# A graph network layer on one core: gather buffers, the first attributes of a layer, and the banks of its completing products

## The chip, the core and the metric

The kernel runs on one core of a Trainium2 chip. The metric is the device time in microseconds (us) of one execution, and the median of three runs stands for it. The core's engines are TensorE (PE; its weight loads are listed as PEld), VectorE (DVE), ScalarE (ACT), GpSimd (POOL) and SyncE (SP). Each has its own instruction stream, and they wait for one another on semaphores. DMAs are issued from SyncE's and ScalarE's queues, and the gathers from GpSimd's.

## What is computed

There are 6250 nodes with 256 values each and 100000 edges, sorted by destination, with 32 attributes and one of three types. Three layers follow one another; at the end each row of input plus result is normalised. Cut to what matters:

```python
ew = edge_attr @ edge_w + edge_b
for l in range(3):
    residual = x
    msg = relu(x[src] * ew)
    out = zeros((n, 256))
    for i in range(3):
        h = segment_sum(msg * rel_masks[i][:, None], dst) * inv_cnt[i][:, None]
        out = out + h @ weights[l, i]
    out = out + x @ roots[l] + biases[l]
    x = residual + relu(out)
x = layernorm(x_in + x)
```

## The kernel before

A first stage looks at the destinations and decides, on the chip, between two paths; the inputs here take `ordered_path`. It splits the edges into 782 tiles of 128 edges. Two tiles are a pair (391 of them), and two pairs a quad. The pairs are worked in the order 64 to 390 and then 63 down to 0, so that the nodes of tiles 0 and 1, which take the edges of the pairs below 64, are finished last.

For a pair, GpSimd gathers the source rows of its two tiles (`gather_pair`, L928, two indirect DMAs of 128 rows of 1 KB). A quad's rows lie in one tile `xs`, which `room` gives out from the pool `rows` of ROWS = 8 buffers. TensorE makes the edge weights `ew_p` from the attributes (L623). VectorE multiplies the rows by them (`weigh`, L645), ScalarE takes the positive part (`bound`, L649), and VectorE builds comparisons of the edges' destinations with places (`one_hot`, L655). TensorE sums the messages by destination and type with them (`reduce`, L665, `h_p`), and VectorE adds the sums to the accumulator `acc` (`add`, L683). When the edges of a tile of 128 nodes are through, `node_mul` (L711) multiplies its sums by the layer's weights and `node_end` (L742 to L762) puts the result together with the root term in `x_root`. In layers 0 and 1 it writes the new rows to `x_mid` in DRAM (L747), from which the next layer gathers; in layer 2 they go to the output.

The order is written out by hand: the loop `for it in range(-11, max(starts) + 7)` issues for each step the pieces of many pairs at different distances. The step's gather is that of the pair AHEAD = 9 places on, `make_ew` that of 4 on, `weigh` that of 3 on, `reduce` its own. The scheduler keeps this order on each engine, so that only the semaphores set when an instruction begins.

The seam between two layers has pieces of its own. FIRST = 6 pairs of the next layer are gathered ahead (`gather_early`, 12 gathers), while node tile 0 of this layer isn't there yet: its rows are zero in `x_mid`. `complete` (L637 to L639) adds the missing rows in the next layer. It multiplies a comparison `came` of the source numbers with the 128 nodes of tile 0 by that tile's rows, and adds the product to `xs`; it does so once for each of the two pairs of the three quads. The 13th gather of a layer and all after it read `x_mid` with tile 0 in it, and so wait for its write. That write in turn overwrites what the early gathers read, and waits for them. In the first layer the six pairs are gathered from the input before the choice of path.

The attributes of eight pairs (a group) are one tile `at` of a pool of three. Layer 0 makes them by transposing `edge_attr` (`turn`, L607, `keep_attrs`, L615) and stores them in `at_all` (`store_at`, L599); layers 1 and 2 load them from there (`load_at`, L563, 512 KB each) on SyncE's queue. The first two groups of the next layer are loaded at the steps U and U + 1, where U = 391 is the number of pairs. The last `store_at` of layer 0 is issued at step U - 5, and the loads of the next layer's root matrix and biases (`load_root`) at U - 10.

The root terms (`root_turn`, L688, to `root_keep`, L699) are made some steps ahead of a node tile's turn, and kept in `x_root`, ROOTS = 24 places of 256 values for each partition. The place of the j-th node tile by turn is j modulo 24. PSUM has eight banks; the pools `o_p` and `r_p` have one each, and `h_p` and `ew_p` the rest with, in layer 0, `turn_p`. `complete` uses `o_p` for both of its products. `r_p` serves the root terms, and the second half of node tiles 0 and 1.

Of the kernel before, what the change touches and what calls it, by code (L numbers as in the profile page):

```python
# [8 lines left out]
F32 = mybir.dt.float32  # L9
# [430 lines left out]


@with_exitstack
def ordered_path(ctx, tc, x, edge_attr, weights, roots, biases, edge_w, edge_b, out, src, src_i, seg, place_i, consts, rows,
                 first_rows, node_i):


# [4 lines left out]
    P = 128  # L451
    N, D = x.shape
    E, A = edge_attr.shape
    L, R = weights.shape[:2]
# [3 lines left out]
    U = T // 2  # L458
# [14 lines left out]
    ident, ones, iota_w = consts  # L473
# [6 lines left out]
    big = ctx.enter_context(tc.tile_pool(name="big", bufs=1))  # L480
# [3 lines left out]
        nc.scalar.dma_start(ew_sb[row + A:row + A1, :], edge_b[None, :])  # L484

    x_all = big.tile([P, NT, D], F32, name="x_all")
    x_root = big.tile([P, ROOTS, D], F32, name="x_root")


    acc = big.tile([P, DC + 1, R, ASIDE + 2 * P + WIN], F32, name="acc")  # L490
# [23 lines left out]
    came_i = came.bitcast(I32)  # L514

    edge = ctx.enter_context(tc.tile_pool(name="edge", bufs=2))
    wpool = ctx.enter_context(tc.tile_pool(name="wpool", bufs=1))
    o_pool = ctx.enter_context(tc.tile_pool(name="o_p", bufs=1, space=PSUM))
    r_pool = ctx.enter_context(tc.tile_pool(name="r_p", bufs=1, space=PSUM))

    groups = list(dict.fromkeys(u // 4 for u in order))
    at_groups = list(dict.fromkeys(u // GROUP for u in order))
# [34 lines left out]
    def pairs_in(g):  # L557
        return min(GROUP, U - GROUP * g)

    def load_at(l, g):  # L560
        at = edge.tile([P, GROUP, P], F32, name="at", bufs=3)
        if l > 0:
            nc.sync.dma_start(at[:, :pairs_in(g)].rearrange("p k e -> p (k e)"), at_all[g, :, :pairs_in(g) * P])  # L563
        return at

    def find_came():
        e = 2 * P * order[0]
        nc.scalar.dma_start(came_i.rearrange("p t e -> p (t e)"),
                            src[e:e + 2 * FIRST * P][None, :].to_broadcast([P, 2 * FIRST * P]))
        for t in range(2 * FIRST):  # L570
            nc.vector.tensor_scalar(came[:, t, :], came_i[:, t, :], node_i[:, 0:1], None, op0=ALU.is_equal)

    def layer(l, r_sb, b_sb, ats, early, pools):
# [13 lines left out]
        r_next, ats_next, early_next = (None, None), {}, {}  # L587

        def gather(u):
            p = order.index(u)  # L590
            if p < FIRST:
                xs[u // 2] = early[u // 2]
            else:
                if first_of(p, 2):
                    xs[u // 2] = room(rows, D)
                gather_pair(nc, xs[u // 2], x_rows, src_i, u)
# [4 lines left out]
        def pairs_of(q):  # L601
            return range(min(2, U - 2 * q))
# [24 lines left out]
        def gather_early(p):  # L627
            u = order[p]
            if first_of(p, 2):
                early_next[u // 2] = room(rows, D)  # L630
            gather_pair(nc, early_next[u // 2], x_mid[l], src_i, u)

        def complete(q):
            for k in pairs_of(q):
                rest = o_pool.tile([P, 2, D], F32, name="o_p")
                for i in range(2):
                    nc.tensor.matmul(rest[:, i, :], came[:, 4 * q + 2 * k + i - 2 * order[0], :], x_all[:, 0, :],  # L637
                                     start=True, stop=True)
                nc.vector.tensor_add(xs[q][:, k], rest, xs[q][:, k])  # L639
# [132 lines left out]

        node_at = {s: c for c, s in enumerate(starts)}
        turns_of = [node_at[s] for s in sorted(node_at)]
        at_root = {c: j % ROOTS for j, c in enumerate(turns_of)}
        root_at = {}

        for j, c in enumerate(turns_of):
# [5 lines left out]
        for it in range(-11, max(starts) + 7):  # L784
            def pair(k):
                return order[it + k] if 0 <= it + k < U else None
            if pair(AHEAD) is not None:
                gather(pair(AHEAD))
            if l < L - 1 and 0 <= it + AHEAD - U < FIRST:
                gather_early(it + AHEAD - U)  # L790
            if l == 0 and it == 20:
                find_came()
            if l == 0 and pair(11) is not None and first_of(it + 11, 4):
                load_attrs(pair(11) // 4)
            if l > 0 and pair(AHEAD) is not None and pair(AHEAD) // GROUP not in ats:
                ats[pair(AHEAD) // GROUP] = load_at(l, pair(AHEAD) // GROUP)
            if l == 0 and it >= -4 and (it + 4) % 20 == 0 and (it + 4) // 20 * 6 < NT - 1:
                load_x((it + 4) // 20 * 6)
            if it == 10:
                nc.sync.dma_start(w_sb, weights[l].rearrange("r (c p) e -> p (r c) e", p=P))  # L800
            if l == L - 1 and it + 2 in root_at:
                load_x0(root_at[it + 2])
            if l < L - 1 and it == U - 10:
                r_next = load_root(l + 1)
            if l < L - 1 and U <= it < U + 2:
                ats_next[at_groups[it - U]] = load_at(l + 1, at_groups[it - U])

            if pair(4) is not None and first_of(it + 4, 2):
                make_ew(pair(4) // 2)
            if pair(0) is not None:  # L810
                reduce(pair(0))
            if pair(-LAG) is not None:
                add(pair(-LAG))
            if pair(3) is not None and first_of(it + 3, 2):
                if l > 0 and it + 3 < FIRST:
                    complete(pair(3) // 2)
                weigh(pair(3) // 2)
                bound(pair(3) // 2)
            if l == 0:

                for k, work in ((6, keep_attrs), (7, turn)):
                    if pair(k) is not None and first_of(it + k, 2):
                        work(pair(k) // 2)
                if pair(4) is not None and last_of(it + 4, GROUP):
                    store_at(pair(4) // GROUP)
            if it in root_at:
                root_turn(root_at[it])
            if it - 1 in root_at:
                root_turned(root_at[it - 1])
            if it - 2 in root_at:  # L830
                root_mul(root_at[it - 2])
            if it - 3 in root_at:
                root_keep(root_at[it - 3])
            if it == moved:
                move()
            if it - 2 == moved:
                clear(P)
            if it + 1 in node_at and slot_of(node_at[it + 1]) == 0:
                wrap()
            if it in node_at:  # L840
                node_mul(node_at[it], 0)
            if it - 1 in node_at:
                node_end(node_at[it - 1], 0)
            if it - 2 in node_at:
                node_mul(node_at[it - 2], 1)
            if it - 3 in node_at:
                node_end(node_at[it - 3], 1)
                clear(slot_of(node_at[it - 3]))
            if it - 4 in node_at and l == L - 1:
                deviate(node_at[it - 4])  # L850
            if it - 5 in node_at and l == L - 1:
                norm(node_at[it - 5])
            if pair(2) is not None and first_of(it + 2, 2):
                one_hot(pair(2) // 2)
# [15 lines left out]
ROOTS = 24  # L870
GROUP = 8
ROWS = 8
FIRST = 6
# [47 lines left out]
def room(rows, D):  # L921

    return rows.tile([128, 2, 2, D], F32, name="xs", bufs=ROWS)
# [10 lines left out]
def kernel(ctx, tc, x, src, dst, edge_attr, edge_type, weights, roots, biases, edge_w,  # L934
# [4 lines left out]
    P = 128  # L939
    N, D = x.shape  # L940
# [7 lines left out]
    U = T // 2  # L948
# [3 lines left out]
    keep = ctx.enter_context(tc.tile_pool(name="keep", bufs=1))  # L952
    ident = keep.tile([P, P], F32, name="ident_o")
    make_identity(nc, ident)
    ones = keep.tile([1, P], F32, name="ones_o")
    nc.vector.memset(ones, 1.0)
    iota_w = keep.tile([P, WK], F32, name="iota_w")
    nc.gpsimd.iota(iota_w, pattern=[[1, WK]], base=0, channel_multiplier=0,
                   allow_small_or_imprecise_dtypes=True)
    node_i = keep.tile([P, 1], F32, name="node_i")  # L960
    nc.gpsimd.iota(node_i, pattern=[[0, 1]], base=0, channel_multiplier=1, allow_small_or_imprecise_dtypes=True)
    src_i = keep.tile([P, TC], I32, name="src_io")
    seg = keep.tile([P, TC], F32, name="seg_o")
    place_i = keep.tile([1, (U + 1) // 2], I32, name="place_i")
    flag = keep.tile([1, 1], I32, name="flag")
    rows = ctx.enter_context(tc.tile_pool(name="rows", bufs=ROWS))

    with tc.tile_pool(name="look", bufs=1) as look, tc.tile_pool(name="look_p", bufs=2, space=PSUM) as look_p, \
            tc.manual_schedule():
        full, rest = divmod(E, P * J)  # L970
# [46 lines left out]
        first_rows = {}  # L1017
        for u in schedule(N, E, 1)[0][:FIRST]:
            if u // 2 not in first_rows:
                first_rows[u // 2] = room(rows, D)  # L1020
            gather_pair(nc, first_rows[u // 2], x, src_i, u)
        dst_t = by_tile("dst")

# [47 lines left out]
    unordered = nc.values_load(flag[0:1, 0:1], min_val=0, max_val=1)  # L1071
    with tc.If(unordered == 0):
        ordered_path(tc, x, edge_attr, weights, roots, biases, edge_w, edge_b, out, src, src_i, seg, place_i,
                     (ident, ones, iota_w), rows, first_rows, node_i)
    with tc.If(unordered > 0):
        general_path(tc, x, src, dst, edge_attr, edge_type, weights, roots, biases, edge_w, edge_b, out)

# [25 lines left out]
```

## Time and profile before

| | us |
|---|---|
| median of 3 runs | 3021.46 (3019.87 to 3021.53) |
| the profiled execution, its own time | 3018.21 |
| its span, first to last instruction | 3016.4 |
| TensorE busy | 2789.6 (92%) |
| GpSimd busy | 2236.2 (74%) |
| VectorE busy | 2080.6 (69%) |
| ScalarE busy | 987.1 (33%) |
| mean granted TensorE clock | 0.942 of full speed |

The profile is of one execution. Its page gives the busy time of each engine, the span in 40 slices with the granted TensorE clock, the chain of work that ended last, and the costliest groups of instructions: line, engine, operation, output<-inputs, count, then the busy time, the mean of one in ns, the idle time ahead of it on its engine, and what ended most of that. "issue" there means that the trace shows nothing that was waited for. The timeline lists instructions in order: start, duration, engine, line, what they write and read, how many are merged (x4), and in brackets the idle time before and what ended it. SPq is an instruction of SyncE's queue that issues a DMA. Most instructions of TensorE are listed in pieces, so that a product in float32 counts as two. The layers run to about 1020, about 2010 and the end.

The waits are also told by who waited for whom. Over the span, ScalarE's L649 waited 1792.3 us for VectorE's L645, L645 waited 362.0 us for gathers from `x_mid` and 97.6 us for gathers from the input, and TensorE's L623 waited 149.2 us for L645.

### The profile page before, as it was taken

The numbers are of one execution on the slowest core, as the hardware profiler recorded it, in microseconds if no ns is written. First come the engines' busy times: TensorE is split into PE (matmuls) and PEld (weight loads), VectorE is DVE, ScalarE is ACT, GpSimd is POOL, SyncE is SP. The second block draws the span as 40 slices with busy tenths as digits, with TensorE's granted clock in tenths as the row PEclk, the third lists the DMA queues.
The fourth block names the chain that finished last, engine by engine and source line by source line (L and its number), as shares of the span: only waits on it lengthen the run. The fifth ranks groups of instructions, "written<-read, shape, count | busy, mean of one in ns | idle before, by whom it ended". The sixth has DMA issues, their size and how long they took to land.

```text
span 3016.4 us, 55782 instructions
## 1 busy us (share of the span) xinstructions
PE 2789.6 (92%) x18114; PEld 2252.3 (75%) x18114; DVE 2080.6 (69%) x5865; ACT 987.1 (33%) x1354; POOL 2236.2 (74%) x2355
## 2 busy tenths in 40 slices
PE   6899999999999889999999999889999999999997
PEld 5777878888877667777777777667777777777775
DVE  6676767777776556666666667556667777877765
ACT  4444444444444222222222222212222222322221
POOL 6777777777777677777777777767777777777775
PEclk9999999999999899999999999878999999999888
DMA  5655555555555444444444445434554444444443
GB/s 154 176 162 161 166 165 151 149 158 156 159 156 145 144 125 137 139 132 140 134 142 144 144 137 149 151 116 140 151 149 146 147 147 149 142 144 144 135 139 97
DMA packets 274682, 438.87 MB, mean 145 GB/s; under 512 B 145004, under 2 KB 180032, under 8 KB 274384
## 3 DMA queue, kind: packets, MB, share of 16 engines
q0 software_dynamic: 112608, 307.65, 35.1%
q1 hardware_dynamic: 154720, 119.64, 13.4%
q10 hardware_dynamic: 7056, 7.92, 0.9%
q8 instruction: 149, 2.44, 0.3%
q14 instruction: 149, 1.22, 0.1%
HBM read 389.94 MB, written 45.09 MB: 144 GB/s over the span
## 4 chain that ended last, share of the span: by engine, by line
PE 56%; DMA 16%; POOL 10%; issue 8%; DVE 7%; ACT 2%; DVEq 0%; ACTq 0%; POOLq 0%; SPq 0%
PE h_p L665 25%; PE ew_p L623 16%; DMA xs<-x_mid,src_io 12%; POOL xs L928 10%; PE o_p L711 9%; DVE xs L645 4%; DMA xs<-in_x_dram,src_io 4%; PE r_p L696 3%; PE turn_p L607 1%; ACT xs L649 1%; DVE x_root L742 1%; DVE acc L683 1%; PE r_p L688 1%; PE o_p L637 0%; PE o_p L715 0%
## 5 line engine op out<-in xcount | busy, mean ns | idle before, releaser
L928 POOL DMA_INDIRECT xs<-x_mid,src_io x1564 | 1488.9, 952 | 503.5 <-issue 416.8
L665 PEld LDWEIGHTS h_p<-oh,xs 128*128 128x128 f32 x9384 | 1214.2, 204 | 245.9 <-issue 190.0
L665 PE MATMUL h_p<-oh,xs 128*128 128x120 f32 x9384 | 1346.3, 295 | 28.2 <-DVE acc L683 12.5
L649 ACT ACTIVATE xs<-xs 128x1024 f32<-128x1024 f32 x588 | 620.2, 1055 | 1857.3 <-DVE xs L645 1792.3
L645 DVE TENSOR_TENSOR xs<-ew_p,xs 128x512 f32<-128x512 f32 x1176 | 753.2, 682 | 558.1 <-DMA xs<-x_mid,src_io 362.0
L623 PE MATMUL ew_p<-ew_sb,at 33*128 33x256 f32 x4692 | 861.0, 418 | 151.3 <-DVE xs L645 149.2
L928 POOL DMA_INDIRECT xs<-in_x_dram,src_io x782 | 745.5, 953 | 255.3 <-issue 198.9
L623 PEld LDWEIGHTS ew_p<-ew_sb,at 33*128 33x128 f32 x4692 | 502.5, 191 | 393.8 <-DVE xs L645 192.1
L683 DVE TENSOR_TENSOR acc<-h_p,acc 128x240 f32 (+1 forms) x1173 | 517.7, 441 | 209.7 <-PE h_p L665 125.3
L655 DVE TENSOR_SCALAR oh<-iota_w,seg_o 128x120 f32<-128x120 f32 x2346 | 512.9, 293 | 0.0
L711 PE MATMUL o_p<-w_sb,acc 128*128 128x256 f32 (+1 forms) x1716 | 442.4, 395 | 4.9 <-DVE acc L683 4.9
L711 PEld LDWEIGHTS o_p<-w_sb,acc 128*128 128x128 f32 (+1 forms) x1716 | 319.1, 198 | 41.7 <-DVE acc L683 6.3
L742 DVE SCALAR_TENSOR_TENSOR x_root<-o_p,inv,x_root 128x256 f32<-128x256 f32 (+1 forms) x429 | 205.7, 480 | 47.0 <-PE o_p L711 39.4
L696 PE MATMUL r_p<-r_sb,t_s 128*128 128x256 f32 x588 | 160.7, 397 | 0.1
L659 ACT ACTIVATE oh_b<-oh 128x480 bf16<-128x480 f32 x196 | 117.9, 602 | 101.3 <-DVE oh L655 99.6
L728 ACT ACTIVATE acc<-zero_o 128x768 f32<-128x768 f32 (+1 forms) x150 | 140.5, 937 | 29.1 <-PE r_p L711 19.1
L696 PEld LDWEIGHTS r_p<-r_sb,t_s 128*128 128x128 f32 x588 | 106.6, 202 | 9.2 <-ACT t_s L692 0.3
L665 PE MATMUL h_p<-oh_b,full_ones 128*128 128x120 bf16 x782 | 107.5, 220 | 0.0
L607 PE MATMUL turn_p<-ident_o,an 128*128 128x128 f32 x391 | 79.4, 286 | 10.7 <-DMA an<-in_edge_attr_dram 6.1
L665 PEld LDWEIGHTS <-full_ones 128*128 128x128 bf16 x782 | 81.9, 105 | 2.5
L699 DVE TENSOR_TENSOR x_root<-r_p,b_sb 128x256 f32<-128x256 f32 x147 | 61.1, 416 | 24.0 <-PE r_p L696 19.5
L615 ACT ACTIVATE at<-turn_p 128x256 f32<-128x256 f32 x196 | 71.7, 366 | 2.7 <-PE turn_p L607 2.7
(93 smaller groups left out, 526.6 us busy)
## 6 DMA issues: line engine op xcount, KB each, us to landing
at<-at_all SPq DMA_DIRECT2D x96, 512.0 KB
xs<-x_mid,src_io POOLq DMA_INDIRECT x1564
at_all<-at SPq DMA_DIRECT2D x48, 512.0 KB
xs<-in_x_dram,src_io POOLq DMA_INDIRECT x782
an<-in_edge_attr_dram SPq DMA_DIRECT2D x97, 128.0 KB
x_mid<-x_all SPq DMA_DIRECT2D x96, 128.0 KB
x_all<-in_x_dram ACTq DMA_DIRECT2D x8, 768.0 KB
x<-in_x_dram SPq DMA_DIRECT2D x48, 128.0 KB
```

The lines of the kernel that those rows point to most:

```text
L623: nc.tensor.matmul(ew_ps[q][i][:, k, :], ats[2 * q // GROUP][i * UP:i * UP + A1, (2 * q + k) % GROUP, :], ew_sb[i * UP:i * UP + A1, :], st ...
L645: nc.vector.tensor_mul(there, ew_ps[q][i][:, :n, :], there)
L649: nc.scalar.activation(there, there, AF.Relu)
L655: nc.vector.tensor_scalar(ohs[q][:, t, :], iota_w, seg[:, 4 * q + t:4 * q + t + 1], None, op0=ALU.is_equal)
L659: nc.scalar.activation(oh_bs[q][:, :n], ohs[q][:, :n], AF.Copy)
L665: nc.tensor.matmul(h_ps[u][:, d, :], xs[u // 2][:, u % 2, i, d * P:(d + 1) * P] if d < DC else full_ones, (ohs if d < DC else oh_bs)[u // ...
L683: nc.vector.tensor_tensor(there, h_ps[u][:, :CH].rearrange("p c (r w) -> p c r w", r=R), there, op=ALU.add)
L696: nc.tensor.matmul(rs[c][:, 1, :], t_ss[c][:, d, :], r_sb[:, d, :], start=(d == 0), stop=(d == DC - 1))
L711: nc.tensor.matmul(o_p[:n, j, :], acc[:, d, r, slot:slot + n], w_sb[:, r * DC + d, :], start=(d == 0), stop=(d == DC - 1))
L728: nc.scalar.activation(acc[:, :CH, :, slot:slot + P], zero[:, :, None, None].to_broadcast([P, CH, R, P]), AF.Copy)
L742: nc.vector.scalar_tensor_tensor(root, o_p[:n, j, :], inv[:n, c, r:r + 1], root, op0=ALU.mult, op1=ALU.add)
L928: nc.gpsimd.indirect_dma_start(out=xs[:, u % 2, i, :], out_offset=None, in_=x_rows[:, :], in_offset=bass.IndirectOffsetOnAxis(ap=src_i[:, ...
```

## The change

There are three parts.

The pool `rows` is opened inside `ordered_path`, behind the choice of path, and no longer ahead of it. The rows of the first six pairs, gathered ahead of the choice, go to the places 0 to 11 of `x_root`, which for that is made ahead of the choice; the root terms of layer 0 start at place 12. In the program that is built, the rooms given out behind the choice were five addresses in turn before, and are eight in turn after.

The first two groups of attributes of the next layer are loaded at the steps U - 10 and U - 9. In SyncE's queue they thereby pass the last `store_at` of layer 0. The order of the queue at the second seam is unchanged.

The second product of `complete` uses the bank of `r_p`.

```diff
-    x_root = big.tile([P, ROOTS, D], F32, name="x_root")
...
+    rows = ctx.enter_context(tc.tile_pool(name="rows", bufs=ROWS))
...
         def complete(q):
             for k in pairs_of(q):
-                rest = o_pool.tile([P, 2, D], F32, name="o_p")
+
+                rest = (r_pool if k else o_pool).tile([P, 2, D], F32, name="r_p" if k else "o_p")
...
-        at_root = {c: j % ROOTS for j, c in enumerate(turns_of)}
+        at_root = {c: (j + 2 * FIRST) % ROOTS for j, c in enumerate(turns_of)}
...
-            if l < L - 1 and U <= it < U + 2:
-                ats_next[at_groups[it - U]] = load_at(l + 1, at_groups[it - U])
+            if l < L - 1 and U - 10 <= it < U - 8:
+                ats_next[at_groups[it - U + 10]] = load_at(l + 1, at_groups[it - U + 10])
...
-    rows = ctx.enter_context(tc.tile_pool(name="rows", bufs=ROWS))
+
+    x_root = keep.tile([P, ROOTS, D], F32, name="x_root")
...
         for u in schedule(N, E, 1)[0][:FIRST]:
             if u // 2 not in first_rows:
-                first_rows[u // 2] = room(rows, D)
+                j = 4 * len(first_rows)
+                first_rows[u // 2] = x_root[:, j:j + 4, :].rearrange("p (k i) d -> p k i d", k=2)
             gather_pair(nc, first_rows[u // 2], x, src_i, u)
```

More of the change, by code (lines that the diff above doesn't have):

```diff
@@ L442, in ordered_path @@
 @with_exitstack
-def ordered_path(ctx, tc, x, edge_attr, weights, roots, biases, edge_w, edge_b, out, src, src_i, seg, place_i, consts, rows,
+def ordered_path(ctx, tc, x, edge_attr, weights, roots, biases, edge_w, edge_b, out, src, src_i, seg, place_i, consts, x_root,
                  first_rows, node_i):
@@ L1073 @@
         ordered_path(tc, x, edge_attr, weights, roots, biases, edge_w, edge_b, out, src, src_i, seg, place_i,
-                     (ident, ones, iota_w), rows, first_rows, node_i)
+                     (ident, ones, iota_w), x_root, first_rows, node_i)
     with tc.If(unordered > 0):
```

## The prediction

> **What bounds the kernel now.** I read the page's engine table and its costliest groups first, then GpSimd's own timeline over the whole span, then the waits in stretches of 50 us, and last the timeline of all engines around every gap found on GpSimd.
>
> TensorE is busy 92% of the span and GpSimd 74%, so the table points at TensorE. The groups correct that:
>
> ```profile
> L928 POOL DMA_INDIRECT xs<-x_mid,src_io x1564 | 1488.9, 952 | 503.5 <-issue 416.8
> L928 POOL DMA_INDIRECT xs<-in_x_dram,src_io x782 | 745.5, 953 | 255.3 <-issue 198.9
> ```
>
> A gather occupies GpSimd for 0.95 us, and there are 2346 of them (782 per layer). The idle time beside them, 758.8 us, is put down to "issue", that is to nothing that was waited for. GpSimd's timeline shows what that is:
>
> ```profile
> 501.10 0.95 POOL L928 DMA_INDIRECT xs<-in_x_dram,src_io  x1 [0.30 <-issue]
> 502.35 0.95 POOL L928 DMA_INDIRECT xs<-in_x_dram,src_io  x1 [0.30 <-issue]
> ```
>
> Columns: start, duration, instruction, idle before it. One gather starts every 1.25 us, with 0.30 us between two that no other engine sets. 2346 x 1.25 = 2934 of 3016.4 us: GpSimd works back to back, and what is left is 10.9 us before the first gather, 21.9 us after the start of the last (2994.49; the last products and the output follow), and the places where GpSimd stood still. These are all that exceed one more idle microsecond, apart from the first:
>
> ```profile
> 57.41 0.95 POOL L928 DMA_INDIRECT xs<-in_x_dram,src_io  x1 [6.42 <-issue]
> 94.84 1.60 POOL L928 DMA_INDIRECT xs<-in_x_dram,src_io  x1 [2.64 <-issue]
> 1023.17 0.94 POOL L928 DMA_INDIRECT xs<-x_mid,src_io  x1 [5.00 <-DMA x_mid<-x_all]
> 1038.50 0.95 POOL L928 DMA_INDIRECT xs<-x_mid,src_io  x1 [5.61 <-issue]
> 1045.92 1.00 POOL L928 DMA_INDIRECT xs<-x_mid,src_io  x1 [2.71 <-issue]
> 2017.28 0.94 POOL L928 DMA_INDIRECT xs<-x_mid,src_io  x1 [4.31 <-DMA x_mid<-x_all]
> 2029.28 0.94 POOL L928 DMA_INDIRECT xs<-x_mid,src_io  x1 [2.27 <-issue]
> 2041.19 0.94 POOL L928 DMA_INDIRECT xs<-x_mid,src_io  x1 [7.21 <-issue]
> 2844.82 0.94 POOL L928 DMA_INDIRECT xs<-x_mid,src_io  x1 [1.44 <-issue]
> ```
>
> Two kinds stand here. 1023.17 and 2017.28 wait for the last node tile's rows to be written. The others wait for a room, though the page says "issue". The seam shows it by counting: 12 gathers were made ahead (3 rooms), 8 more start from 1023.17 to 1031.94 (2 rooms), then GpSimd stops. Five rooms are in use, not eight. The built program agrees: the three rooms filled ahead of the branch are never given out again behind it, and the first gather of quad q waits for the last h_p product of quad q-5. Only the start differs, where 3+5 were free: 32 gathers, then the stop before 57.41.
>
> The layer ends are gather-bound too: VectorE's product at 1008.45 had waited 4.09 us for the last gather of layer 0, the one at 1999.96 2.38 us for that of layer 1, and the chain that ended last goes through the last gathers of layer 2. So a stall of GpSimd is worth its length at the end, if the engines behind it can follow.
>
> **The rooms: eight instead of five.** In the built program of after, every gather that waited for quad q-5 waits for quad q-8: 12 gathers, 15 us, later. At the start it is 3 places in x_root and 8 rooms, 44 gathers instead of 32. Nothing is added: same instructions, same bytes, and x_root's places 0 to 11 are free long before a root sum is put there (roots begin at place 12).
>
> What goes, as idle time less the normal 0.30:
> - start: 6.1 + 2.3 = 8.4. The second follows VectorE's stop for `came` (5.40 us for its load, 2.45 for its 12 comparisons).
> - first seam: 5.3 + 2.4 = 7.7.
> - second seam: 2.0 + 6.9 = 8.9.
> - 2844.82, and two small ones at 2850.08 (0.55) and 2854.02 (0.50): 1.14 + 0.25 + 0.20 = 1.6.
>
> Sum 26.6. Is 15 us enough cover? After the first stop, the gather that needs what was freed at 57.41 comes at 50.05 + 13 x 1.25 = 66.3: 9 us to spare. What was freed at 94.84 is needed 15 us later, less the 8.4 us that GpSimd is now ahead: 6.6 to spare. First seam: 1023.17 + 20 x 1.25 = 1048.2 for what was free at 1038.5, and 1053.2 against 1045.9. Second: 2042.3 against 2029.3, 2047.3 against 2041.2. The smallest margin is 6.1 us. Next late is thus not a room but the rows of the last tile.
>
> A rule of the skill speaks against a gain: Perfetto Trace Analysis, "What 'DMA-bound' means", calls a sequencer row that is solid with DMA slices bound by descriptor generation, where only larger descriptors help. By it alone deeper buffers bring 0. The row is solid in its 1.25 us steps, and I follow the rule there: none of the 2934 us is touched. But the row isn't solid where GpSimd waits for a room, and those 26.6 us are what depth can reach.
>
> Can the others follow? In layers 1 and 2 yes: behind the seam TensorE makes a quad in 3.3 to 3.9 us (h_p groups start at 1043.13, 1046.39, 1050.30, 1053.56), against 5.0 of GpSimd, before node products. Layer 0 is tight: TensorE is busy 75.00 of 75 us from 300 to 375. What it starves there is its wait for VectorE's weighing at L623: summed over the stretches from 50 to 1000 it is 24.8 us, 11.1 of it by 400. The lead of 8.4 us fits in three times over, so I carry it whole; the lower bound of what arrives is 0.
>
> **The wait for the last rows.** It stays. At the second seam x_all was ready at 2009.61, but:
>
> ```profile
> 2014.83 0.32 SPq L747 DMA_DIRECT2D x_mid<-x_all  x1
> ```
>
> The write may not start before the last early gather (begun 2012.02) has read: 2.81 us, then 2.45 to the next gather. Start to start 5.26, a stall of 4.0 that GpSimd makes for itself. At the first seam it is 4.7, as x_all came at 1020.67, after the early gathers had landed (1017.23 + 2.8 = 1020.0). At most 0.7 can go there.
>
> **The attributes.** In SyncE's queue the two loads of 512 KB pass only one instruction, the last at_all store of layer 0; at the second seam the order is the same as before (its second load went out at 1977.00 already). At the first seam:
>
> ```profile
> 999.74 0.34 SPq L599 DMA_DIRECT2D at_all<-at  x1
> 1000.18 1.21 SPq L563 DMA_DIRECT2D at<-at_all  x2
> ```
>
> They were held behind that store, and met the last gathers: the one begun at 1002.22 was used only at 1008.45, 6.2 us later, against 2.9 in the final chain. Moved, they wait for a buffer whose last ew product is 13 steps of some 2.6 us before the layer's last h_p products at 1014, about 980. They hold the store and nothing else behind them, since that store waits for ScalarE until 999.7 anyway. They now cost 3.3 us of landing in mid-stream; TensorE runs a quad in 3.6 us there (995.33 to 998.93), so it regains this in 3 quads, 15 us, before the end. The last gather lands 3.3 us sooner, and x_all comes before the early gathers have landed: 0.7 gained. If the cover were gone, 3.3 lost. I take 0.7.
>
> **The two banks.** The completing products of a quad were one after the other:
>
> ```profile
> 1020.81 1.10 PE L637 MATMUL o_p<-x_all,came 128*128 128x256 f32 x4 [0.58 <-DVE x_all L745]
> 1021.95 0.69 DVE L639 TENSOR_TENSOR xs<-o_p,xs 128x512 f32<-128x512 f32 x1 [1.28 <-PE o_p L637]
> 1022.70 1.13 PE L637 MATMUL o_p<-x_all,came 128*128 128x256 f32 x4 [0.78 <-DVE xs L639]
> 1023.87 0.69 DVE L639 TENSOR_TENSOR xs<-o_p,xs 128x512 f32<-128x512 f32 x1 [1.22 <-PE o_p L637]
> ```
>
> With the second bank the second product runs during the first addition, and the pair is done about 0.8 us sooner. The skill (Perfetto Trace Analysis, "Matmuls") wants independent groups in rotating banks so that evacuation overlaps; by it the gain is 6 quads x 0.8 = 5. The row that sets the end says 0: TensorE's work at the seam lies under GpSimd's next 20 gathers. I take 0; between 0 and -5 for the range. The borrowed bank r_p is next wanted by the root transpose at 1044.90, after the third quad's additions: no new wait. There is no loss here.
>
> **The sum.** 26.6 + 0.7 = 27.3. The profiled execution took 3018.21 (span 3016.4); the median of the runs is 3.25 above it. 3018.2 - 27.3 = 2990.9 as profiled, 3021.5 - 27.3 = 2994 as a median.
>
> **Rivals.** *Layer 0 can't follow.* TensorE is nearly full there, so the 8.4 us turn into a longer wait for x_mid at the first seam, and the 0.7 fall away. For it: 75.00 of 75 busy. Against: the 24.8 us of starving, and the 4.09 us wait at the end. 3021.5 - 18.2 = 3003.
>
> *The rooms weren't the wait.* If the "issue" gaps had another cause, nothing changes: 3021. Against it are the counts of 20 and 32 gathers.
>
> *Slower: TensorE's clock in layer 0.* The granted clock there averages 0.974 over the 75 us stretches. TensorE starves 2.5% of the layer; below a mean of about 0.95 it is the bound instead of GpSimd, and each further 0.01 costs some 10 us of 975. The change is slower by 6 us from a mean of about 0.915; at 0.91 the time is 3021.5 - 27.3 + 41 = 3035. For it: stretches of 0.83 and 0.89 at the layer's end. Against: half-speed products follow idle, as at 1010.23 (4.35 us idle, then 1.96 us for eight products that took 1.15 warm), and as the skill says (TensorE: Matmul & The Clock Gate, "What's actually happening": an idle window drops the clock to half). The change takes idle time away.
>
> **The numbers.** The forecast 2994 has 0.78 (0.76 of this counts as faster, the rest as within the bound), layer 0 not following 0.12, no change 0.04, slower 0.06. A run's noise is 1.5 us; a measurement of this kernel can tell 0.2%, 6 us, from no change. Low: 2994 - 5 (banks) - 1.5 = 2988. High: the first rival at 3003 + 1 = 3004. Faster 0.76 + 0.12 = 0.88, same 0.06, slower 0.06.
>
> **What would show it.** Right: GpSimd without gaps at the start, behind both seams and at 2844; two gaps of about 4 us left, both before the 13th gather of a layer; the loads near 970 to 980; the last gather of layer 0 used about 3 us after its start. Wrong: a gap at the seam of 8 us or more (layer 0 didn't follow), gaps called "issue" where rooms are free, or a layer 0 clock below 0.95.

## The result, and the profile after

| | before | after |
|---|---|---|
| median, same chip, 6 runs each | 3020.66 (3015.11 to 3024.66) | 2995.62 (2995.00 to 2996.61) |
| the profiled execution | 3018.21 | 2995.39 |
| its span | 3016.4 | 2993.6 |
| start of the first and of the last gather | 10.93, 2994.49 | 10.97, 2971.72 |
| TensorE, GpSimd, VectorE busy | 92%, 74%, 69% | 93%, 75%, 70% |
| mean granted TensorE clock | 0.942 | 0.942 |

The ratio is 0.9916, with a 95% interval of 0.9904 to 0.9929: 25 us less, between 21 and 29. The forecast was 2994.

I read after in the order in which I had read before. First the page's costliest groups: GpSimd's work is the same (1491.9 and 735.2 us, 0.95 us a gather), and what shrank is the idle time beside it. Twelve of the 782 gathers from the input now write `x_root`, so that 770 are left in that group.

```profile
L929 POOL DMA_INDIRECT xs<-x_mid,src_io x1564 | 1491.9, 954 | 484.9 <-issue 397.5
...
L929 POOL DMA_INDIRECT xs<-in_x_dram,src_io x770 | 735.2, 955 | 234.8 <-issue 189.3
```

Then GpSimd's timeline of after over the whole span. Of the stops of over one more microsecond that before had, these two are left; both are the 13th gather of a layer, which waits for tile 0's rows:

```profile
1015.31 0.95 POOL L929 DMA_INDIRECT xs<-x_mid,src_io  x1 [4.41 <-DMA x_mid<-x_all]
...
2003.43 0.95 POOL L929 DMA_INDIRECT xs<-x_mid,src_io  x1 [4.36 <-PE o_p L638]
```

The releaser in brackets is the profile's guess for the last of several semaphores. The second says `o_p`, yet it is the same wait: SyncE issues that tile's write at 2000.97, and 2.46 us later the gather begins.

The sum closes. Take all steps from one gather to the next of 1.45 us or more, and add what exceeds 1.25 us: 38.5 us in before, 11.1 us in after (the stall, from here on). So 27.4 us of stall are gone, and the last gather starts 22.8 us sooner. The other 4.6 us went into the ordinary steps, whose mean is 1.2559 us in before and 1.2579 us in after: 0.0020 us on 2331 steps.

Then SyncE's timeline at the first seam. The loads of attributes go out at 972.04, ahead of the last store of layer 0, and the write of the last tile still waits, until 1012.84, though `x_all` was ready at 1008.53:

```profile
972.04 5.35 SPq L563 DMA_DIRECT2D at<-at_all  x2
991.41 0.32 SPq L599 DMA_DIRECT2D at_all<-at  x1
1012.84 0.32 SPq L748 DMA_DIRECT2D x_mid<-x_all  x1
```

VectorE's timeline shows what the clear queue does to the last gather of layer 0, begun at 994.88. Its rows are used 2.9 us after that, where before they were used after 6.2:

```profile
997.77 1.29 DVE L646 TENSOR_TENSOR xs<-ew_p,xs 128x512 f32<-128x512 f32 x2 [1.46 <-DMA xs<-in_x_dram,src_io]
```

The completing products of a quad overlap now; the timeline of TensorE and VectorE at the first seam:

```profile
1008.68 1.10 PE L638 MATMUL o_p<-x_all,came 128*128 128x256 f32 x4 [0.58 <-DVE x_all L746]
1009.62 1.03 PE L638 MATMUL r_p<-x_all,came 128*128 128x256 f32 x4
1009.82 0.69 DVE L640 TENSOR_TENSOR xs<-o_p,xs 128x512 f32<-128x512 f32 x1 [1.29 <-PE o_p L638]
1010.69 0.69 DVE L640 TENSOR_TENSOR xs<-r_p,xs 128x512 f32<-128x512 f32 x1 [0.17 <-PE r_p L638]
```

From the start of the first product to the end of the second addition it is 2.70 us (1008.68 to 1011.38), against 3.75 in before (1020.81 to 1024.56). The second product starts while VectorE still waits for the first, and not after the first addition.

### The profile page after: what moved, and what is told of

It reads as the page before. It is cut to its first block, busy times and chain, and to the rows that moved or that the text cites. A ratio compares the mean times of both kernels' runs of the same rounds, so it can differ in the third digit from the quotient of the medians.

```text
span 2993.6 us, 55665 instructions
## 1 busy us (share of the span) xinstructions
PE 2780.0 (93%) x18114; PEld 2253.5 (75%) x18114; DVE 2082.5 (70%) x5865; ACT 988.0 (33%) x1354; POOL 2240.4 (75%) x2355
## 4 chain that ended last, share of the span: by engine, by line
PE 54%; DMA 15%; POOL 14%; issue 10%; DVE 5%; ACT 1%; DVEq 0%; POOLq 0%; ACTq 0%
PE h_p L666 25%; PE ew_p L623 15%; POOL xs L929 14%; DMA xs<-x_mid,src_io 11%; PE o_p L712 9%; DVE xs L646 3%; DMA xs<-in_x_dram,src_io 3%; PE r_p L697 3%; PE turn_p L607 1%; ACT xs L650 1%; PE r_p L689 1%; PE o_p L716 0%; DVE x_root L743 0%; DVE acc L684 0%; ACT acc L729 0%
## 5 line engine op out<-in xcount | busy, mean ns | idle before, releaser
L929 POOL DMA_INDIRECT xs<-x_mid,src_io x1564 | 1491.9, 954 | 484.9 <-issue 397.5
L666 PE MATMUL h_p<-oh,xs 128*128 128x120 f32 x9336 | 1343.9, 296 | 22.0 <-DVE acc L684 11.4
L650 ACT ACTIVATE xs<-xs 128x1024 f32<-128x1024 f32 (+1 forms) x585 | 617.1, 1055 | 1819.9 <-DVE xs L646 1772.3
L623 PE MATMUL ew_p<-ew_sb,at 33*128 33x256 f32 x4692 | 846.6, 417 | 149.9 <-DVE xs L646 148.2
L929 POOL DMA_INDIRECT xs<-in_x_dram,src_io x770 | 735.2, 955 | 234.8 <-issue 189.3
L623 PEld LDWEIGHTS ew_p<-ew_sb,at 33*128 33x128 f32 x4692 | 495.2, 191 | 384.8 <-DVE xs L646 181.0
```

What stands on the lines that cost most here:

```text
L623: nc.tensor.matmul(ew_ps[q][i][:, k, :], ats[2 * q // GROUP][i * UP:i * UP + A1, (2 * q + k) % GROUP, :], ew_sb[i * UP:i * UP + A1, :], st ...
L650: nc.scalar.activation(there, there, AF.Relu)
L666: nc.tensor.matmul(h_ps[u][:, d, :], xs[u // 2][:, u % 2, i, d * P:(d + 1) * P] if d < DC else full_ones, (ohs if d < DC else oh_bs)[u // ...
L929: nc.gpsimd.indirect_dma_start(out=xs[:, u % 2, i, :], out_offset=None, in_=x_rows[:, :], in_offset=bass.IndirectOffsetOnAxis(ap=src_i[:, ...
```

## The experiments

The theory: GpSimd's step of 1.25 us is the bound, its stops for a room and for `x_mid` are lost one for one, and the rooms alone make the gain. The rivals: the loads or the banks carry a part of it, or depth works by something else than those stops. The runs fell on three chips; each is compared only with runs of before on its own chip.

| run | its chip's before, median | median | ratio (95%) |
|---|---|---|---|
| rooms_only | 3762.8 (34 runs) | 3784.46 | 1.0063 (1.0043 to 1.0082) |
| loads_only | 3762.8 | 3763.72 | 1.0009 (0.9986 to 1.0031) |
| banks_only | 3762.8 | 3752.61 | 0.9968 (0.9942 to 0.9993) |
| loads_banks | 3762.8 | 3752.33 | 0.9976 (0.9956 to 0.9996) |
| rooms_6 | 3013.53 (11 runs) | 2994.53 | 0.9933 (0.9917 to 0.9948) |
| rooms_7 | 3013.53 | 2991.18 | 0.9921 (0.9905 to 0.9936) |
| two_copies | 3013.53 | 2984.78 | 0.9901 (0.9884 to 0.9917) |
| fewer_gathers | 3013.53 | 2885.51 | 0.9571 (0.9551 to 0.9591) |
| rooms_only_b | 3012.97 (23 runs) | 2992.24 | 0.9933 (0.9916 to 0.9950) |
| loads_banks_b | 3012.97 | 3002.34 | 0.9965 (0.9952 to 0.9979) |
| banks_only_b | 3012.97 | 3003.23 | 0.9971 (0.9958 to 0.9984) |
| after_b | 3012.97 | 2991.69 | 0.9933 (0.9916 to 0.9951) |

### The parts by themselves, on a chip that is 25% slower

`rooms_only` is the change without the edits of the loads and of the banks, `loads_only` and `banks_only` are one of those edits on before, `loads_banks` both:

```diff
-            if l < L - 1 and U <= it < U + 2:
-                ats_next[at_groups[it - U]] = load_at(l + 1, at_groups[it - U])
+            if l < L - 1 and U - 10 <= it < U - 8:
+                ats_next[at_groups[it - U + 10]] = load_at(l + 1, at_groups[it - U + 10])
...
-                rest = o_pool.tile([P, 2, D], F32, name="o_p")
+                rest = (r_pool if k else o_pool).tile([P, 2, D], F32, name="r_p" if k else "o_p")
```

The first hunk is `loads_only`, the second `banks_only`.

> The eight buffers and the places in x_root alone; the two loads of attributes and the completing products stay as before. My theory: GpSimd sets the end, and its stalls for rooms are the whole gain, so this runs within 2 us of the changed kernel: about 2996, with two gaps of 4.0 to 4.7 us left before the 13th gather of layers 1 and 2. The rival that the gain comes of the earlier loads or the two banks: above 3010.

> The two loads of attributes at the steps U - 10 and U - 9 alone. My theory: only the first seam changes; the last gather of layer 0 is used about 3 us after its start and not 6.2, which is worth at most 0.7 us there: 3020, not told from the kernel before. The rival that the loads held up the seam: 3017 or less.

> The second completing product in r_p's bank alone, with five rooms in use. My theory: here TensorE's and VectorE's work at the seam isn't covered, since GpSimd waits for the first two quads; the first is done 0.8 us sooner and the second 1.7, so 2 to 5 us in all: 3017, near the edge of what is measurable. The rival, by which the banks are covered in any case: 3021.

> The loads and the banks without the rooms: all of the change but its first part. My theory: 3 to 6 us, as the sum of the two alone, about 3016; added to the rooms alone it would give 7 us more than the changed kernel shows, since with eight rooms the same work is covered. The rival that the parts are independent: the rooms alone must then be at about 3001.

These four fell on a chip on which before itself takes 3763 us, and none of the times expected can hold there. Of the differences, that of `loads_only` is the none that was expected; `banks_only` and `loads_banks` take 10.2 and 10.5 us off, more than the 2 to 5 and 3 to 6 expected, which comes again below. The rooms alone are even 0.6% slower. The instructions are as long as elsewhere (a gather 0.95 us, 1.25 us from start to start; eight `ew_p` products about 1.13 us where the clock is full), but GpSimd stops about every sixth gather, for 2 us on average: some 370 stops of 770 to 790 us in all in each of the four. That is about the 750 us by which this chip is slower. GpSimd is not the bound on that chip, so a room more only lets it run further ahead and wait longer where it can't: in `rooms_only` the 13th gather of layer 1 waits for 22.46 us,

```profile
1356.48 0.94 POOL L929 DMA_INDIRECT xs<-x_mid,src_io  x1 [22.46 <-DMA x_mid<-x_all]
```

and in `loads_only`, with five rooms, for 9.51 us:

```profile
1345.74 0.94 POOL L928 DMA_INDIRECT xs<-x_mid,src_io  x1 [9.51 <-DMA x_mid<-x_all]
```

The difference, 13 us, is about the 15 us that twelve gathers take. So a condition that the prediction took as given, that GpSimd is what the others wait for, can fall away with the chip. What holds the engines behind it is not settled: in `loads_only` VectorE stands for 470 us ahead of L683 and L645 with "remote" as the releaser (a name that no wait has in before and after), and 0.844 of the clock is granted. Nor is it settled why eight rooms cost 0.6% rather than nothing. The whole change was not run on that chip.

### Fewer rooms, and no wait for the last rows

`rooms_6` and `rooms_7` are after with another number of rooms:

```diff
-ROWS = 8
+ROWS = 6
```

> The changed kernel with ROWS = 6, so 5 us of cover and not 15. My theory: of each group of stalls at most 5 us go: 5 of 8.4 at the start, 5 of 7.7 and 5 of 8.9 at the seams (where the second bank adds 1 to 2 each), all of 1.6 late: some 17 to 20 us, 3002 to 3005, with stalls again at the start and behind the seams. The rival that it needs all eight rooms: near 3015. The rival that the first extra room is all: 2996.

> The changed kernel with ROWS = 7, 10 us of cover. My theory, from a smallest margin of 6.1 us with eight, of which a room takes 5: no stall for a room is left, 2996, as the changed kernel. The rival that each room brings its share: 2999 to 3001.

Six rooms took 19.0 us off, seven 22.4. The 19.0 lies in the 17 to 20 expected, but not for all of the reasons given: stops were expected behind the seams too, and `rooms_6` has none there beyond the waits for `x_mid`. With six, two of the stops at the start come back, smaller; GpSimd's timeline of `rooms_6`:

```profile
58.55 0.94 POOL L929 DMA_INDIRECT xs<-in_x_dram,src_io  x1 [2.70 <-issue]
...
94.17 1.64 POOL L929 DMA_INDIRECT xs<-in_x_dram,src_io  x1 [0.93 <-issue]
```

Less the normal 0.30 they are 2.40 + 0.63 = 3.0 us, and the run is 3.35 us above `rooms_7`, which has no stop for a room. Those are the stops that before had as 6.42 and 2.64 at the same places with five rooms. One room more is worth four gathers, 5 us of cover, and it is the stop that is paid, not the number of rooms. That the eighth adds nothing is read from `rooms_7` having no stop left, and from its ratio, 0.9921, beside 0.9916 and 0.9933 for the whole change on other chips; eight rooms were not run on this chip.

`two_copies` is after with the early gathers reading another copy of the rows, so that the last tile's write need not wait for them:

```diff
+    x_early = [dram.tile([N, D], F32, name=f"x_early{l}") for l in range(L - 1)]
...
-    for rows_of in x_mid:
+    for rows_of in x_early:
...
-            gather_pair(nc, early_next[u // 2], x_mid[l], src_i, u)
+            gather_pair(nc, early_next[u // 2], x_early[l], src_i, u)
...
                 nc.sync.dma_start(x_mid[l][c * P:c * P + n, :], x_all[:n, c, :])
+                if c > 0:
+                    nc.sync.dma_start(x_early[l][c * P:c * P + n, :], x_all[:n, c, :])
```

> The changed kernel, and the rows of a layer are written twice to DRAM, once for the early gathers (without node tile 0) and once for the others, so that the write of tile 0 doesn't wait for the early gathers. 96 more writes of 128 KB on SyncE's queue. My theory: GpSimd made those two stalls of 4.1 us for itself; x_all is ready early enough (1008.5 in the changed kernel, gather due at 1011.2), so both go: 2996 - 8 = 2988. The rival that the wait turns to x_all or to the added writes: 2994 to 2998.

It took 28.8 us off its chip's before, 6.4 more than `rooms_7`, which stands in for after there. At the first seam the write follows `x_all` at once (1008.75 after 1008.72) and the gather has 1.88 us of idle time left; at the second it doesn't wait at all. GpSimd's timeline of `two_copies`:

```profile
1011.74 0.95 POOL L932 DMA_INDIRECT xs<-x_mid,src_io  x1 [1.88 <-DMA x_mid<-x_all]
...
1993.17 0.95 POOL L932 DMA_INDIRECT xs<-x_mid,src_io  x1 [0.30 <-issue]
```

Against `rooms_7` (4.16 and 4.04 beyond the step) that is 2.6 + 4.0 = 6.6 us, which is the 6.4. So the wait for the last rows is the one that GpSimd makes for itself, as the prediction had it, at the price of a second write of each node tile but the first. This version beats both kernels.

### Fewer gathers

`fewer_gathers` fetches, in layers 1 and 2, the second tile of every ninth pair (outside the first six) with an ordinary load of 128 successive rows on SyncE's queue instead of a gather, so those pairs work on other rows than the reference's.

```diff
-                gather_pair(nc, xs[u // 2], x_rows, src_i, u)
+                apart = l > 0 and u % 9 == 4
+                gather_pair(nc, xs[u // 2], x_rows, src_i, u, (0,) if apart else (0, 1))
+                if apart:
+                    nc.sync.dma_start(xs[u // 2][:, u % 2, 1, :], x_rows[u * 8:u * 8 + P, :])
```

> The changed kernel, in which 84 gathers of layers 1 and 2 (the second tile of every ninth pair) are left out and replaced by plain loads of 128 rows in a row, the same bytes, on SyncE's queue; the output is not the reference's. My theory: GpSimd's step of 1.25 us is the bound, and 84 x 1.25 = 105 us go: 2891, or 2900 if TensorE is then the bound at places. The rival that TensorE bounds, or the bytes moved: 2990 or more.

84 gathers less are 84 x 1.25 = 105 us; measured against `rooms_7` it is 105.7. The bytes and the work of the other engines are the same, so the bound of after is GpSimd's step itself, not the bytes and not TensorE at 93%.

### The parts again, with the whole change beside them

The edits are those of the first four runs; `after_b` is the change as it stands.

> The change's first part alone (all eight rooms in turn; loads and banks as before), a second time, since the first time it ran on a chip on which the kernel before takes 3763 us. On a chip where it takes 3011 to 3024: my theory (GpSimd's stalls for a room were worth their length) expects 22 to 26 us less than before there, ratio 0.991 to 0.993, x_mid waits of 4 to 5 us as the only gaps on GpSimd, and a last gather about 22 us sooner. The rival that the other two parts made a share of the gain expects less than 18 us. On the slow chip again: ratio 1.004 to 1.008.

> The whole change beside its parts, on the same chip. On a chip where the kernel before takes 3011 to 3024 us: ratio 0.991 to 0.993, and the same as the rooms alone within 3 us. On a chip where it takes 3763 us: my theory (there the landing of the gathers is the bound, not GpSimd's step, and depth buys nothing) expects ratio 1.000 to 1.006; the rival (the stalls for a room are lost there too) expects 0.993 or less.

> The change's third part alone (completing products in two banks, rooms and loads as before), a second time, since the first time it ran on the slower chip. On a chip where the kernel before takes 3011 to 3024 us: my theory expects 0 to 3 us less, as with five rooms the first completed quad frees the room that GpSimd waits for, 0.8 to 0.9 us sooner at each seam. The rule that rotating banks give all their 0.8 us for each of six quads expects 5 us less; no effect at all expects 0 with an interval around it.

> The change's second and third parts (loads of attributes ten steps ahead, completing products in two banks) with the rooms as before, a second time, since the first time it ran on the slower chip. On a chip where the kernel before takes 3011 to 3024 us: my theory expects 0 to 4 us less: 0.7 from the first seam, and up to 0.9 for each seam, because five rooms make GpSimd wait for the completed quads, so that the bank's 0.8 us can lie on the path there; stalls of 5.0 to 5.6 and 2 to 3 us behind the first seam stay. The rival (they carry a share of the change's 25 us) expects 8 us less or more.

On this chip the rooms alone do as much as the whole change: 20.7 us off against 21.3, where 22 to 26 were expected of them. GpSimd's timeline of `rooms_only_b` has the two waits for `x_mid` and no other stop of a microsecond:

```profile
1014.11 0.94 POOL L929 DMA_INDIRECT xs<-x_mid,src_io  x1 [4.40 <-DMA x_mid<-x_all]
...
2000.44 0.94 POOL L929 DMA_INDIRECT xs<-x_mid,src_io  x1 [4.31 <-DMA x_mid<-x_all]
```

But what I had expected of the other two runs fell. The banks alone, with five rooms, took 9.7 us off (4.8 to 12.7 by the interval), where I had expected 0 to 3 and the rule of rotating banks 5; with the loads it was 10.6, in the range that I had given to the rival. The stops for a room at the second seam, 1.97 and 6.91 us in before, are gone in `banks_only_b`, though it has no room more, and at the first seam 5.31 and 2.41 have become one of 2.57:

```profile
1039.72 0.95 POOL L928 DMA_INDIRECT xs<-x_mid,src_io  x1 [2.87 <-ACT t_s L692]
```

TensorE's timeline shows why. In before, from the first completing product of the second seam to the first sums:

```profile
2009.67 1.13 PE L637 MATMUL o_p<-x_all,came 128*128 128x256 f32 x4 [0.49 <-DVE x_all L745]
2011.64 1.13 PE L637 MATMUL o_p<-x_all,came 128*128 128x256 f32 x4 [0.84 <-DVE xs L639]
2012.70 0.70 PE L623 MATMUL ew_p<-ew_sb,at 33*128 33x256 f32 x2
2014.28 2.07 PE L623 MATMUL ew_p<-ew_sb,at 33*128 33x256 f32 x6 [0.88 <-DVE xs L645]
2016.28 2.07 PE L637 MATMUL o_p<-x_all,came 128*128 128x256 f32 x4
2019.19 2.07 PE L637 MATMUL o_p<-x_all,came 128*128 128x256 f32 x4 [0.84 <-DVE xs L639]
2021.20 1.22 PE L623 MATMUL ew_p<-ew_sb,at 33*128 33x256 f32 x2
2022.77 2.07 PE L623 MATMUL ew_p<-ew_sb,at 33*128 33x256 f32 x6 [0.36 <-DVE xs L645]
2024.77 3.77 PE L665 MATMUL h_p<-oh,xs 128*128 128x120 f32 x16
```

and in `banks_only_b` the same work, whose first completing product began at 2004.01, from the second `ew_p` group on:

```profile
2007.60 1.10 PE L623 MATMUL ew_p<-ew_sb,at 33*128 33x256 f32 x6 [0.97 <-DVE xs L645]
2008.63 1.13 PE L637 MATMUL o_p<-x_all,came 128*128 128x256 f32 x4
2009.60 1.03 PE L637 MATMUL r_p<-x_all,came 128*128 128x256 f32 x4
2010.56 0.70 PE L623 MATMUL ew_p<-ew_sb,at 33*128 33x256 f32 x2
2012.22 1.10 PE L623 MATMUL ew_p<-ew_sb,at 33*128 33x256 f32 x6 [0.97 <-DVE xs L645]
2013.25 2.04 PE L665 MATMUL h_p<-oh,xs 128*128 128x120 f32 x16
```

From 2014.28 on each product of before takes twice as long: 2.07 for 1.10 and 1.03, 3.77 for 2.04. The first sums of a quad begin 15.10 us after the first completing product in before, 9.24 in `banks_only_b` (from 2004.01), and the second quad's come 11.91 us after those, against 6.41. That is 5.9 us sooner for the first room and 11.4 for the second: more than the stops of 2.0 and 6.9. The windows of 30 us from the seam give the granted clock (the third number from the end; before it is each engine's busy time), for before

```profile
2009.00:2039.00 30.00, 25.40 (x77) 16.57 (x76) 13.03 (x31) 3.96 (x4) 14.43 (x16) 0.58 0.35 103
```

for `banks_only_b`

```profile
2004.00:2034.00 30.00, 26.91 (x166) 20.62 (x166) 19.88 (x52) 6.89 (x8) 19.84 (x21) 1.00 0.50 153
```

and for `rooms_only_b`

```profile
1996.00:2026.00 30.00, 25.39 (x103) 16.82 (x99) 15.04 (x38) 4.65 (x6) 19.60 (x22) 0.72 0.41 121
```

0.58, 1.00 and 0.72. Of the 5.9 us by which the first sums come sooner, the bank's own part is the two waits of 0.84 us ahead of second products, 1.7 us; the rest, some 4 us, is the clock (an estimate from these lines).

The first seams differ less. From their first completing product on, before had 0.83 and `banks_only_b` still 0.89, though its second products don't wait there either:

```profile
1020.81:1050.81 30.00, 25.45 (x122) 18.05 (x123) 16.55 (x43) 5.56 (x6) 15.22 (x16) 0.83 0.43 132
...
1018.00:1048.00 30.00, 27.01 (x149) 21.18 (x150) 20.01 (x52) 7.00 (x8) 17.85 (x19) 0.89 0.49 148
```

Taken so over all traces of the faster chips, the clock was 0.57 to 0.83 in the four seams with one bank (before and `rooms_only_b`), and 0.83 to 1.00 in the 16 seams with two, in five of them 1.00. The first sums began 13.2 to 15.8 us after the first completing product with one bank, and 9.2 to 11.2 with two. So the second bank shortens the work behind the seam, and the clock is higher with it, though it does not always stay full. That the missing waits of 0.84 us are what keeps it up fits these traces and is not shown: nothing was run that has the waits without the shared bank.

With eight rooms the slow clock is still there (0.72), but the next 20 gathers cover it: `rooms_only_b` and `after_b` differ by 0.6 us. The parts' gains, 20.7 and 10.6, therefore don't add to the 21.3 of the whole, because both remove the same stops behind the seams. The loads by themselves are 0.9 us between `banks_only_b` and `loads_banks_b`, less than the intervals can tell from none.

One sum over all these traces: the stall on GpSimd, as added above, against the time of the same profiled execution. Before had 38.5 us of stall and took 3018.21 us.

| run | stall in the trace | less than before by | profiled execution | less than before by |
|---|---|---|---|---|
| banks_only_b | 24.2 | 14.3 | 3001.97 | 16.2 |
| loads_banks_b | 20.3 | 18.2 | 3000.78 | 17.4 |
| rooms_only_b | 12.1 | 26.4 | 2995.02 | 23.2 |
| after_b | 10.9 | 27.6 | 2992.26 | 26.0 |

The two agree within 3.2 us. The one trace of before is of another chip, and 5.2 us above this chip's median of before, so the gains of the medians (9.7, 10.6, 20.7 and 21.3) are smaller than these.

## Why the prediction was right, step by step

- **The bound.** Right: 84 gathers less were worth 105.7 us, where 1.25 us each make 105. (A slip in the reading: of the 758.8 us of idle time beside the gathers the page puts 615.7 down to "issue", not all.)
- **The rooms, 26.6 us.** Right in place and size. All nine stops for a room are gone. The sum of all stalls fell by 27.4 us, where 27.3 were predicted for the rooms and the first seam together. That the rule on a solid row holds for the 2934 us and not for the stops was right too.
- **Layer 0 can follow.** Right: the first early gather of layer 1 begins 7.3 us sooner (996.13 for 1003.47), of 8.4. TensorE took it up out of its idle time: busy 100.00 of 100 us from 100 to 200, where it was 97.42 before. The granted clock in the four stretches of 250 us up to 1000 was 0.97, 0.97, 1.00 and 0.95, not the 0.915 at which the slower case begins.
- **x_mid, 4.0 us at each seam.** Right: 4.11 and 4.05 beyond the step. At the first seam that is 0.59 less than before, of the 0.7 predicted.
- **The loads, 0.7 us.** The timing is right: they are issued at 972.04, and the last gather is used 2.9 us after its start. But the 0.59 us at the first seam can't be credited to them: `rooms_only_b`, which loads at the old steps and uses its last gather 4.7 us after the start, waits there for 4.10 us beyond the step, as after does (4.11), and so does `banks_only_b`. Alone the loads can't be told from nothing.
- **The banks, 0.** Right for the whole change, since the 20 gathers cover them. But the price named for the case without that cover, 0.8 us for each of six quads and 5 us in all, was too small: with five rooms it measured 9.7 us. The term that was mis-sized is the 0.8: it counted the wait and not the time at half clock, which at the second seam was the longer part. The same holds for the stops in the sum: I took the 16.6 us behind the seams as a property of five rooms. They belong to five rooms and one shared bank together; with two banks and five rooms 2.6 us of them are left.
- **As a median.** 2994 forecast, 2995.6 measured; that they are so close is in part luck. As profiled, 2990.9 was forecast and 2995.4 measured: the stall went as predicted, and 4.6 us went into the ordinary steps. That is not the change's doing, since the steps average 1.2554 in `rooms_7`, 1.2555 in `rooms_only_b` and 1.2561 in `after_b`. The two medians differ by 25.0 us on this chip and by 21.3 on the last (15 to 25 by the interval), not by 27.3. Before is the kernel that varies: on the last chip its runs lie between 3007 and 3025, those of after (fewer runs) between 2989 and 2995, so the 1.5 us that I took as a run's noise was too little. That the seams of before sometimes keep the full clock, and so stop GpSimd for less, would make this spread; it was not shown, as before has one trace.

## What to carry over

Where one engine paces a kernel, sum its stops in its own timeline and test each one's cause by counting buffers; "issue" as the releaser can hide a wait for a buffer, and depth pays for exactly the stops it covers and no more. Two edits that take away the same stop don't add, so run each alone and both together before one of them is credited. And first ask whether that engine is the pace on the chip at hand: where it wasn't, the same rooms brought a loss of 0.6%.

## What was not expected of the hardware

A row of short waits cost TensorE its clock. The waits in before at the second seam are 0.49, 0.84 and 0.88 us; the Trainium skill (TensorE: Matmul & The Clock Gate, "Why this matters for your kernels") asks only that no gap exceed about 3 us. By that rule the clock would have held; the trace says 0.50 from 2020 to 2030. The same page's "A second HAM failure mode: psum-queue depth-cycling" tells of a clock that swings where short idles between groups of products are frequent, and agrees with the trace. In `banks_only_b` waits of 0.97 us, one to a quad, left the clock at 1.00 at the second seam and took it to 0.89 at the first, so it isn't the length of a single wait that decides; what does is open. And in before it stayed low under load: from 2020 to 2030 TensorE was busy for 9.64 of 10 us, at half speed throughout.

One chip of those used was 25% slower with the same instructions at the same lengths (3763 against 3013 us for before). The rooms cost 0.6% there and gain 0.7% elsewhere; the second bank took 10 us off on both (10.2 and 9.7).
